# A smaller first wave and a reordered start in a two-layer feed-forward and convolution kernel with 4-bit weights

## The chip, the cores and the metric

The kernel runs on one core of a Trainium2 chip. The metric is the device time of one execution in microseconds (us); several executions of one kernel agree to within a fraction of a per cent. The core has five engines that run side by side, each with its own queue of instructions that it works through in order: TensorE (PE in the profile; its weight loads are PEld), VectorE (DVE), ScalarE (ACT), GpSimd (POOL) and SyncE (SP). SP, ACT and POOL also issue DMA transfers, and such an issue stands in the engine's queue like any instruction: if it waits, what is behind it waits too.

## The reference

The input is 2048 rows of 1024 numbers. Three residual steps follow each other: half a gated feed-forward layer, a long convolution along each row (an S4 kernel made from small tables), and the same feed-forward layer once more. Each normalises its rows first. The weights of the feed-forward layer are 4-bit numbers, eight to a word, with a zero point and a scale for each group of 128 input rows.

```python
def _layernorm(x, axis=-1, eps=1e-05):
    m = jnp.mean(x, axis=axis, keepdims=True)
    v = jnp.var(x, axis=axis, keepdims=True)
    return (x - m) / jnp.sqrt(v + eps)

# in _dequant: 4-bit weights, W[k,n] = scales[g,n] * (w4[k,n] - (z4[g,n]+1))
w = (qw[:, None, :] >> shifts[None, :, None] & MAXQ).reshape(-1, qweight.shape[1])
z = ((qz[:, :, None] >> shifts[None, None, :] & MAXQ) + 1).reshape(qzeros.shape[0], -1)
return (w.astype(scales.dtype) - z[g_idx].astype(scales.dtype)) * s

# in _L0_ffn_ref: 1024 -> 2752 (gate and up) -> 1024 (down)
h = jax.nn.silu(xf @ Wg) * (xf @ Wu)
out = h @ Wd

# the whole
x = x + 0.5 * ffn(_layernorm(x))
x = x + s4_convolution(_layernorm(x))
x = x + 0.5 * ffn(_layernorm(x))
```

## The kernel before

The 2048 rows are four blocks of 512, and the two feed-forward layers make eight jobs of one block and one layer (`JOBS`, L1260). A job has two stages, `gate_up` and `down`. In `gate_up` the 2752 columns of gate and up are taken in pairs of 128 columns (one of gate, one of up): 21 pairs and a half one. Pairs are grouped in waves (`WAVES`, L37): five waves of three pairs and three of two, the last with the half pair. A wave holds one PSUM bank of 128x512 for each of its six (or four) units and goes through the eight groups of 128 input rows; wave and group are a step (`STEPS`), 64 in all. In a step every unit gets two products, the high part of the rows (`xTh`) and the low part (`xTl`), and then its bank is multiplied in place by the ratio of two groups' scales (`scaled`, L596). ScalarE does the gate units, VectorE the up units; in job 0 ScalarE takes one up unit too in every fourth step. I call that an eviction. At the wave's end come silu, the product of gate and up, and the split of the result in two parts (`gated`, L653).

Weights are unpacked once, in job 0. For a wave `fetch` loads the packed words (tile `raw`), `fetch_zeros` reads zero points spread over rows from a DRAM table (`z`), `split` makes two tiles of bytes (`even` and `raw`, L453 and L454), `take_zeros` adds the zero points (L461 and L462), and `dequantize` (L474) casts one of eight interleaved rows at a time to a tile `q` and stores it to the DRAM tensor `wq` of the wave. From there each step's weights come back as bytes (`load_bytes`, L550, four steps ahead) and are cast to 32 bits (`make_weights`, L567, three steps ahead) into `w_up`. The very first step's bytes are put together directly in the tile `first_tile`, by eight small DMAs on POOL's queue. `zero_words` (L263) and `zero_points` (L277) load the packed zero points (`zq`), unpack them (`zi`), and store the table (`ztab` to `z_dram` or `zd_dram`).

Before job 0 stands `start` (L1379): it loads the first four row tiles `x_0` to `x_3`, finds mean and variance (`moments`, `deviations`), unpacks wave 0, normalises the first half of the columns (`less_mean` and `by_deviation` on ScalarE, `turn` with transposes on TensorE, `xTh` on ScalarE, `xTl` on VectorE, L242), and makes the scales of the first three pairs (`scales`, L316). `in_order_of_writing` (L140) holds the instructions of ACT, VectorE and SP in the order in which `start` has them. The other work is placed by a scheduler when the kernel is built, which can move instructions on an engine past each other.

Side work hangs on steps: the dictionaries `up` and `dn` name what is written out at the start of which step. In job 0 the second half of the rows (`second_half`) hangs on steps 0 to 3, the scales of pairs 3 to 8 on step 2, and the unpacking of wave w on the steps from 8w-12 on. In the jobs that follow a first layer (jobs 1, 2, 5 and 6) the block before gets its last additions at steps 0 to 3 (`back`, L709), its moments and deviations at steps 4 and 5, and its convolution from step 8 (in job 1 from step 38). In jobs 3 and 4 the next block's moments and deviations hang on steps 44 and 45.

Pools matter in one place: `qpool` has four buffers, and a tile `q` is free again only when both of its DMAs have landed.

Of the kernel before, what the change touches and what calls it, by code (L numbers as in the profile page):

```python
# [36 lines left out]
WAVES = [list(range(3 * w, 3 * w + 3)) for w in range(5)] + [[15, 16], [17, 18], [19, 20]]  # L37
# [17 lines left out]
def macaron_s4_kernel(  # L55
# [207 lines left out]
    def zero_words(which):  # L263

        if which:
            n = HID // 8 // SEGD
            z = t2("zq_1").bitcast(I32)[: GD * SEGD, :n]
            nc.sync.dma_start(z, down_qz.rearrange("g (s n) -> (g s) n", s=SEGD))
            return z
        n = INTER // 8 // SEG  # L270
        z = t2("zq_0").bitcast(I32)[:, :n]
        for i, src in enumerate((gate_qz, up_qz)):
            own = slice(GK * SEG * i, GK * SEG * (i + 1))
            nc.scalar.dma_start(z[own], src.rearrange("g (s n) -> (g s) n", s=SEG))
        return z
# [198 lines left out]
    def dequantize(w, j):  # L474

        q = qpool.tile([P, width_of(w)], I8, tag="q", name=f"q_{w}_{j}")
        engine = nc.vector if w == 0 and j % 3 < 2 else nc.gpsimd
        engine.tensor_copy(q, packed[w][j % 2][:, j // 2, :])
        dst = w_q[w].rearrange("(r j) n -> j r n", j=8)[j]
        if w == 0:  # L480
            nc.gpsimd.dma_start(first_tile[j:P:8], q[: P // 8])
        nc.sync.dma_start(dst, q)
        if j == 7:
            packed.pop(w)

# [81 lines left out]
    def make_weights(i):  # L567
# [5 lines left out]
        elif j == 0 and stage == "up" and s % GK in (1, 2, 5):  # L573
            nc.scalar.copy(t, b)
        else:
            nc.gpsimd.tensor_copy(t, b)  # L576
# [3 lines left out]
    def next_weights():  # L580
        i = at_use[0]
        at_use[0] += 1
        for k in range(LOAD) if i == 0 else ():
            load_bytes(k)
        for k in range(MAKE) if i == 0 else ():
# [676 lines left out]
    def fast():  # L1262
        for j, (b, k) in enumerate(JOBS):
# [50 lines left out]
            if j == 0:  # L1314
# [6 lines left out]
                at(up, 40, scales_down)  # L1321
                for t in range(NT):
# [56 lines left out]
    def start():  # L1379
        zeros = zero_words(0)  # L1380
        x[0] = [t4(f"x_0_{t}") for t in range(NT)]
        for t, src in enumerate(rows_of(u, 0)):
            (nc.sync, nc.scalar)[t // 2].dma_start(x[0][t], src)
        fetch(0)
# [4 lines left out]
        zero_points(0, zeros)  # L1389
        fetch_zeros(0)  # L1390
        fetch_zeros(1)

        def then(t, m):
            means[t] = m
            less_mean(t, 0)
            if t == 2:
                split(0)
# [4 lines left out]
        for i in range(8):  # L1402
            dequantize(0, i)
        for t in range(NT + 1):
            if t < NT:
                by_deviation(t, 0)
            if t:
                turn(0, t - 1, first[t - 1, 0], 0)
        for t in range(NT):
            less_mean(t, 1)  # L1410
        scales(0, 3, srow)
        zero_points(1, zeros_down)
        return rows_next

    srow_next = in_order_of_writing(start, *STARTING)
# [88 lines left out]
```

## Time and profile before

| | |
|---|---|
| median of 3 executions | 2164.68 us (2164.53 to 2165.5) |
| the profiled execution, own time | 2165.84 us |
| its span in the profile | 2164.1 us |
| mean granted TensorE clock | 0.993 |
| PE busy | 2097.0 us, 97% of the span |
| DVE busy | 1723.0 us, 80% |
| ACT busy | 1422.9 us, 66% |
| POOL busy | 1038.7 us, 48% |

The span is the time from the first to the last recorded instruction; the execution's own time has a little around it. A share of busy time is an average over stages with different limits, so the text below reads single stretches: a window of the timeline, or the waits of one engine. In a timeline line the first number is the start in us from the span's start, the second how long the group took, then come engine, source line, operation, what is written from what is read, the shape, and in brackets the idle time before it with what ended it. L numbers are lines of the kernel before.

Where TensorE waits for nothing it takes 0.22 to 0.23 us for each product of 128x128 by 128x512.

### The profile page before, as it was taken

The page shows a single profiled execution, that of the slowest core. Times are in us where ns is not written, and L with a number is a line of the kernel's source. Part 1 is how long each engine was busy: PE and PEld are TensorE (multiplying, and loading weights), DVE is VectorE, ACT ScalarE, POOL GpSimd, SP SyncE. Part 2 cuts the span into 40 slices and gives each one's busy share as a digit, 9 for nine tenths or more (in the row PEclk, how much of TensorE's full clock was granted, in tenths as well). Part 3 has the DMA queues.
Part 4 walks back from the last instruction along what each step waited for, and adds up shares of the span by engine and source line. Part 5 has one row for each costly group of instructions (what it writes and reads, how often), then busy time and mean ns, then how long its engine had stood idle before and what let it go on. Part 6 is the DMA issues. An engine that isn't in the chain of part 4 may idle for free.

```text
span 2164.1 us, 30241 instructions
## 1 busy us (share of the span) xinstructions
PE 2097.0 (97%) x9748; PEld 1429.4 (66%) x9748; DVE 1723.0 (80%) x2831; ACT 1422.9 (66%) x2233; POOL 1038.7 (48%) x1366
## 2 busy tenths in 40 slices
PE   5999899899999999999999999999999999999998
PEld 3555676476867568665776558676686766866576
DVE  7889787778887877778777787878778787777776
ACT  5887677546754677676667767646776467767765
POOL 3868835444345453455335553445534455345642
PEclk9999999999999999999999999999999999999999
DMA  4433321112111311211321121112111121121111
GB/s 141 122 95 116 113 65 42 43 46 80 37 39 51 97 45 46 80 34 33 111 76 42 31 72 35 41 52 74 37 34 40 54 93 44 47 81 36 33 35 57
DMA packets 163543, 132.48 MB, mean 61 GB/s; under 512 B 22252, under 2 KB 151029, under 8 KB 163376
## 3 DMA queue, kind: packets, MB, share of 16 engines
q1 hardware_dynamic: 162528, 129.12, 19.7%
q8 instruction: 79, 1.29, 0.3%
q10 hardware_dynamic: 592, 1.25, 0.2%
q14 instruction: 88, 0.72, 0.1%
q0 software_dynamic: 256, 0.10, 0.0%
HBM read 104.79 MB, written 25.50 MB: 60 GB/s over the span
## 4 chain that ended last, share of the span: by engine, by line
PE 86%; DVE 8%; DMA 2%; POOL 2%; issue 1%; ACT 0%; SPq 0%; DVEq 0%; POOLq 0%; ACTq 0%
PE pg L628 52%; PE po L691 27%; PE pc L993 3%; DVE pg L600 2%; PE pb L713 1%; PE pb L993 1%; DVE po L600 1%; PE pt L219 1%; PE st L219 1%; DVE hf L658 1%; POOL qd L510 1%; DMA raw<-in_L_ffn_up_qweight_dram 0%; PE s_k L915 0%; ACT g L655 0%; DVE hb L674 0%
## 5 line engine op out<-in xcount | busy, mean ns | idle before, releaser
L598 ACT ACTIVATE pg<-pg,rat 128x512 f32<-128x512 f32 x1240 | 786.5, 660 | 435.7 <-PE pg L628 435.0
L600 DVE TENSOR_TENSOR pg<-pg,rat 128x512 f32<-128x512 f32 x1168 | 776.2, 693 | 168.3 <-PE pg L628 163.5
L628 PE MATMUL pg<-xTh,w_up 128*128 128x512 f32 x2752 | 855.1, 438 | 8.3 <-DVE pg L600 6.0
L628 PE MATMUL pg<-xTl,w_up 128*128 128x512 f16 x2752 | 722.8, 383 | 12.4 <-DVE w_up L572 6.6
L576 POOL CAST w_up<-b 128x768 fp32r<-128x768 int8 (+2 forms) x487 | 375.2, 775 | 566.6 <-PE pg L628 454.9
L628 PEld LDWEIGHTS pg<-xTh,w_up 128*128 128x128 f32 x2752 | 519.7, 189 | 185.1 <-DVE pg L600 23.3
L691 PE MATMUL po<-hl,w_down 128*128 128x512 f32 x1344 | 542.7, 406 | 15.5 <-DVE po L600 11.4
L598 ACT ACTIVATE po<-po,ratd 128x512 f32<-128x512 f32 x660 | 431.9, 662 | 167.7 <-PE po L691 167.3
L691 PE MATMUL po<-hh,w_down 128*128 128x512 f32 x1344 | 525.9, 393 | 0.0
L600 DVE TENSOR_TENSOR po<-po,ratd 128x512 f32<-128x512 f32 x620 | 427.1, 697 | 94.1 <-PE po L691 89.9
L628 PEld LDWEIGHTS <-w_up 128*128 128x128 bf16 x2752 | 228.6, 99 | 336.5 <-issue 152.5
L576 POOL CAST w_down<-bd 128x512 fp32r<-128x512 int8 x352 | 222.6, 634 | 417.8 <-PE po L691 357.8
L691 PEld LDWEIGHTS po<-hl,w_down 128*128 128x128 f32 x1344 | 253.9, 189 | 91.9 <-DVE po L600 24.3
L691 PEld LDWEIGHTS po<-hh,w_down 128*128 128x128 f32 x1344 | 254.7, 190 | 45.8
L662 POOL TENSOR_TENSOR hl<-hf,hh 128x512 fp32r<-128x512 f32 x168 | 217.4, 1294 | 8.4
L658 DVE SCALAR_TENSOR_TENSOR hf<-pg,rat,g 128x512 f32<-128x512 f32 x168 | 123.2, 748 | 45.0 <-ACT g L655 39.9
L655 ACT ACTIVATE g<-pg,rat 128x512 f32<-128x512 f32 x168 | 110.8, 687 | 51.2 <-PE pg L628 41.1
L660 POOL CAST hh<-hf 128x512 fp32r<-128x512 f32 x168 | 106.2, 632 | 63.3 <-PE pg L628 37.1
L182 DVE BATCH_NORM_STATS2 stats<-x 128x6 f32<-128x512 f32 x96 | 63.3, 675 | 0.4
L1023 DVE TENSOR_TENSOR x<-x,pc 128x512 f32<-128x512 f32 x32 | 22.0, 686 | 36.4 <-PE pc L993 36.4
L219 PE MATMUL pt<-ident,xn 128*128 128x128 f32 x256 | 43.8, 288 | 7.3 <-ACT xn L1371 7.3
L242 DVE TENSOR_TENSOR xTl<-pt,xTh 128x512 f16<-128x512 f32 x56 | 38.3, 688 | 13.7 <-ACT xTh L241 12.9
(177 smaller groups left out, 1047.8 us busy)
## 6 DMA issues: line engine op xcount, KB each, us to landing
b<-wq SPq DMA_DIRECT2D x319, 96.0 KB
bd<-wdq SPq DMA_DIRECT2D x336, 64.0 KB
x<-in_L_attn_u_dram SPq DMA_DIRECT2D x30, 512.0 KB
b<-wq SPq DMA_DIRECT2D x128, 64.0 KB
xs<-x SPq DMA_DIRECT2D x16, 512.0 KB
x<-xs SPq DMA_DIRECT2D x16, 512.0 KB
out_dram<-x SPq DMA_DIRECT2D x16, 512.0 KB
b<-wq SPq DMA_DIRECT2D x64, 80.0 KB
```

Source lines behind the costliest of these rows:

```text
L182: nc.vector.bn_stats(stats[:, t, i, :], x[b][t][:, bass.ts(i, 512)])
L219: nc.tensor.transpose(ps[:, bass.ts(k, P)], n[:, bass.ts(k, P)], ident)
L576: nc.gpsimd.tensor_copy(t, b)
L598: nc.scalar.activation(dst, src, AF.Copy, scale=sc)
L600: nc.vector.tensor_tensor(dst, src, sc.to_broadcast([P, TB]), ALU.mult)
L628: nc.tensor.matmul(p, weights, (lo, hi)[k][:, g, :], start=(g == 0 and not done), stop=(g == GK - 1 and done), skip_group_check=True,)
L655: nc.scalar.activation(g, pg, AF.Silu, scale=rat[:, 2 * f, GK - 1 :])
L658: nc.vector.scalar_tensor_tensor(hf, pu, last, g, ALU.mult, ALU.mult)
L660: nc.gpsimd.tensor_copy(hi, hf)
L662: nc.gpsimd.tensor_tensor(lo, hf, hi.bitcast(F32), ALU.subtract)
L691: nc.tensor.matmul(ps[c], w[:, bass.ts(c, P)], part, start=(f == 0 and k == 0), stop=(f == NF - 1), skip_group_check=True,)
L993: nc.tensor.matmul(dst, lhsT, rhs, start=start, stop=stop, skip_group_check=True)
```

## The change

The waves are regrouped: the first one now has two pairs, five have three, and the last two have two. Before, the first five had three and the last three had two. Their number stays eight.

In `start` the packed zero points are loaded first, one half on SP's queue and one on ACT's; then the words of wave 0; then the rows, three tiles on SP's queue and one on ACT's (before, two on each, ahead of the words). The zero points of wave 0 are unpacked and its words split before the moments, not around them. A one-element silu right behind the first DMA issues makes ScalarE load its function table there.

Wave 0 is cast by a function of its own, `dequantize_first`: two rows of eight on GpSimd and six on VectorE, as before, but in another order, in pairs that share a tile of the h pool instead of `qpool`; both the small DMAs to `first_tile` and the stores to `wq` go by SP, the latter four instead of eight. The first step's bytes and weights are written at the end of `start`, ahead of the scales; of the next steps' casts, step 1's goes to GpSimd instead of ScalarE. The zero points for down are unpacked at step 12 of job 0 instead of in `start`.

```diff
-WAVES = [list(range(3 * w, 3 * w + 3)) for w in range(5)] + [[15, 16], [17, 18], [19, 20]]
+WAVES = [[0, 1]] + [list(range(3 * w - 1, 3 * w + 2)) for w in range(1, 6)] + [[17, 18], [19, 20]]
...
-        for i, src in enumerate((gate_qz, up_qz)):
+        for i, (src, queue) in enumerate(((gate_qz, nc.sync), (up_qz, nc.scalar))):
             own = slice(GK * SEG * i, GK * SEG * (i + 1))
-            nc.scalar.dma_start(z[own], src.rearrange("g (s n) -> (g s) n", s=SEG))
+            queue.dma_start(z[own], src.rearrange("g (s n) -> (g s) n", s=SEG))
...
-        engine = nc.vector if w == 0 and j % 3 < 2 else nc.gpsimd
-        engine.tensor_copy(q, packed[w][j % 2][:, j // 2, :])
-        dst = w_q[w].rearrange("(r j) n -> j r n", j=8)[j]
-        if w == 0:
-            nc.gpsimd.dma_start(first_tile[j:P:8], q[: P // 8])
-        nc.sync.dma_start(dst, q)
+        nc.gpsimd.tensor_copy(q, packed[w][j % 2][:, j // 2, :])
+        nc.sync.dma_start(w_q[w].rearrange("(r j) n -> j r n", j=8)[j], q)
         if j == 7:
             packed.pop(w)
+
+    def dequantize_first():
+
+        n = width_of(0)
+        dst = w_q[0].rearrange("(r j) n -> r j n", j=8)
+        parts = packed.pop(0)
+        for j in (0, 1, 5, 4):
+            q = t2(f"q_0_{j}").bitcast(I8)[:, : 2 * n].rearrange("p (i n) -> p i n", i=2)
+            for i in range(2):
+                row = j + 2 * i
+                engine = nc.vector if j else nc.gpsimd
+                engine.tensor_copy(q[:, i], parts[j % 2][:, row // 2, :])
+                nc.sync.dma_start(first_tile[row:P:8], q[: P // 8, i])
+            nc.sync.dma_start(dst[:, j : j + 3 : 2], q)
...
-        elif j == 0 and stage == "up" and s % GK in (1, 2, 5):
+        elif j == 0 and stage == "up" and s > 1 and s % GK in (1, 2, 5):
...
-        for k in range(LOAD) if i == 0 else ():
+        for k in range(1, LOAD) if i == 0 else ():
             load_bytes(k)
-        for k in range(MAKE) if i == 0 else ():
+        for k in range(1, MAKE) if i == 0 else ():
             make_weights(k)
...
+                zeros = lambda: zero_points(1, zeros_down)
+                at(up, 12, lambda: in_order_of_writing(zeros, ET.DVE, ET.SP))
...
     def start():
         zeros = zero_words(0)
+        fetch(0)
         x[0] = [t4(f"x_0_{t}") for t in range(NT)]
         for t, src in enumerate(rows_of(u, 0)):
-            (nc.sync, nc.scalar)[t // 2].dma_start(x[0][t], src)
-        fetch(0)
+            (nc.sync, nc.scalar)[t // 3].dma_start(x[0][t], src)
+        warm = small.tile([P, 1], F32, tag="warm", name="warm")
+        nc.gpsimd.memset(warm, 0.0)
+        nc.scalar.activation(warm, warm, AF.Silu)
+        zero_points(0, zeros)
+        split(0)
+        fetch_zeros(0)
         srow = scale_rows(0, 3)
         zeros_down = zero_words(1)
         fetch(1)
         rows_next = scale_rows(3, 9)
-        zero_points(0, zeros)
-        fetch_zeros(0)
         fetch_zeros(1)
 
         def then(t, m):
             means[t] = m
             less_mean(t, 0)
-            if t == 2:
-                split(0)
 
         moments(0, 1, then)
         deviations(0, 1, -LIFT)
         take_zeros(0)
-        for i in range(8):
-            dequantize(0, i)
+        dequantize_first()
         for t in range(NT + 1):
             if t < NT:
                 by_deviation(t, 0)
             if t:
                 turn(0, t - 1, first[t - 1, 0], 0)
+        load_bytes(0)
+        make_weights(0)
         for t in range(NT):
             less_mean(t, 1)
         scales(0, 3, srow)
-        zero_points(1, zeros_down)
-        return rows_next
+        return rows_next, zeros_down
```

More of the change, by code (lines that the diff above doesn't have):

```diff
@@ L1411, in start @@
         scales(0, 3, srow)
[L1412 to L1415 removed]
+        return rows_next, zeros_down
+    srow_next, zeros_down = in_order_of_writing(start, *STARTING)
     x.pop(0)
```

## The prediction

> **What bounds the kernel now.** I read the page's shares first, then the chain of waits, then the two ends of the change: the first 60 us, and the first wave of a later job.
>
> ```profile
> PE 86%; DVE 8%; DMA 2%; POOL 2%; issue 1%; ACT 0%; SPq 0%; DVEq 0%; POOLq 0%; ACTq 0%
> ```
>
> That is the chain that ended last: TensorE carries 86% of the span and VectorE 8%. Outside the start TensorE is the bound, so a change of the start is worth what it lets TensorE begin and keep its pace earlier. The waits of TensorE, then of VectorE, in the first 62 us (total, times, longest):
>
> ```profile
> PE pg L628 <- DVE w_up L572: 6.6, 1, 6.6
> PE pg L628 <- POOL w_up L576: 0.8, 1, 0.8
> ```
> ```profile
> DVE zi L282 <- DMA zq<-in_L_ffn_up_qzeros_dram: 6.4, 1, 6.4
> DVE q L478 <- DMA b<-q: 2.1, 2, 1.6
> ```
>
> The first product waits for its weights, which VectorE casts. VectorE's own timeline (start, duration) says why they are late:
>
> ```profile
> 6.40 0.84 DVE L282 TENSOR_SCALAR zi<-zq 128x43 int32<-128x43 int32 x8 [6.40 <-DMA zq<-in_L_ffn_up_qzeros_dram]
> ...
> 7.71 1.28 DVE L182 BATCH_NORM_STATS2 stats<-x 128x6 f32<-128x512 f32 x2
> ...
> 16.89 0.17 DVE L205 TENSOR_SCALAR r<-r 128x4 f32<-128x4 f32 x1
> 17.07 0.96 DVE L461 TENSOR_TENSOR even<-even,z 128x1536 uint16<-128x1536 uint16 x1
> ...
> 23.62 0.56 DVE L478 COPY q<-even 128x768 int8<-128x768 int8 x1 [1.64 <-DMA b<-q]
> ...
> 25.69 2.47 DVE L242 TENSOR_TENSOR xTl<-pt,xTh 128x512 f16<-128x512 f32 x4
> ...
> 28.51 0.56 DVE L572 CAST w_up<-b 128x768 fp32r<-128x768 int8 x1
> ```
>
> VectorE sits idle until 6.40, waiting for 22 KB of packed zero points, and from there works without a gap but for the 2.1 us at 23-25. After the first product it is still VectorE that sets the pace. Windows over TensorE's products of L628 (length, busy and number), one window for each of the first three waves of 96 products:
>
> ```profile
> 29.10:59.90 30.80, 27.22 (x96) 0.94 0.41 120
> 59.90:83.00 23.10, 22.54 (x97) 1.00 0.42 124
> 83.00:104.70 21.70, 21.70 (x97) 1.00 0.36 103
> ```
>
> The third wave runs at 21.7/96 = 0.226 us a product, TensorE's own pace; the first needs 30.8. The second thing to see is a later job's first wave, in windows over all engines (length; PE, PEld, DVE, ACT, POOL busy):
>
> ```profile
> 1376.00:1392.00 16.00, 16.00 (x75) 9.87 (x72) 15.75 (x38) 10.52 (x18) 4.78 (x6) 1.00 0.12 32
> ```
>
> VectorE is 15.75 of 16 us busy there, beside a TensorE that is never idle: no room is left.
>
> [...] here the last store of `wq` is issued at 25.80 and the load that needs it at 27.82, 2.02 later. [...] the zero points, issued at 0.75 and 1.33 on ACT's queue, come only at 6.40 with a megabyte of rows on SP's queue beside them. [...] the trace has 1.28 us at 10.82 and at 56.34. [...] the cast q<-even took 1.49 us at 18.68 beside VectorE and 0.83 at 24.06.
>
> **The change part by part.**
>
> *Loads.* The two zero-point loads are now first on SP and ACT, then the words (2 x 128 KB instead of 2 x 192), then x_0 to x_2 on SP and x_3 on ACT. With nothing ahead, the zero points cost about the 2 us: at 2.9 instead of 6.4 (estimate). The DMA moved 322 and 353 GB/s in its busiest slices; 2.1 MB of x and 0.26 MB of words at 0.35 MB/us after a start at 1.5 give x_2 at about 8.4, words at 4.3, x_0 at 5.6. VectorE: zero points 1.4 (0.84+0.52) to 4.3, split of 512 columns 0.75 to 5.1, then moments of 1.34 each as rows come: x_2 done at 9.8, x_3 at 11.1, against 14.5. Bounds: 10 if rows come sooner[...]. The 2.55 us of deviations follow: 13.7 against 17.07. z is stored right after 4.3 and read by about 10, so it is not late.
>
> *Casts of the first wave.* take_zeros on 512 columns costs two thirds of 3.5 us, 2.3: to 16.0. Six casts on VectorE stay six, each 0.37 instead of 0.55: 18.3. The 2.1 us of waits for a buffer of `q` go, as four tiles of the h pool hold the results. Then the four xTl, 2.4: 20.7; ScalarE's last xTh lay 6.2 after r, so 19.9, and doesn't hold them. Late next is SP: the 12 stores (8 to `first_tile`, formerly on POOL's queue, and 4 to `wq`) at 0.45 to 0.5 each, the first after POOL's cast at about 15.9, put the last `first_tile` store at 20.6 and the last `wq` store at 21.2. Landing takes 1.7 to 2: 22.4. The cast of the first weights, 0.4, ends at 22.9 (bounds 21.5 and 24.2), against 29.07: 6.2 us earlier. `b` of step 1 is read after the last `wq`, 23.2, lands at 25, and POOL casts it by 25.5; step 0 is 8 products, 1.8 us, and the first eviction waits for the scales anyway, so this costs about nothing.
>
> *First wave.* It shrinks to 64 products, 14.5 us of TensorE. VectorE's work from the first weights to the wave's last eviction, in pitches from the first 60 us: scales 3.4 (both sets now stand ahead of the first eviction), 12 evictions at 0.6, four xTl 2.4, splits and zeros of waves 1 and 2 at 4.4 each, less a last step of 0.6: about 20. Before, the same list had 19 evictions and the zero points of down. So 22.9+20 = 42.9, and about 2.5 more because wave 2's z, issued behind four `wq` stores at about 37, lands near 41.7 with two evictions queued behind that wait (in the trace such a z, issued at 45.33, ended a wait at 49.76). POOL's cast of step 8's weights stands behind the first cast of wave 2, so wave 1 begins near 46.2. Add 32 products at wave 1's 0.24: 96 products done at 53.9 instead of 59.9. **Start: -6.0** (bounds -3.5 and -8.5).
>
> *Zero points of down* move to step 12: 1.2 us of VectorE in wave 1, in pieces of 0.1. VectorE had 20.3 busy of 23 us there, so most is covered: +0.4 (0 to 1.2).
>
> *ACT table.* The load at 10.82 ended before the rows' means were all there, and the one at 56.34 fell where TensorE did not wait: 0. One load for all is enough, since one stands in the built program.
>
> *Order of waves, all 8 jobs.* Products stay 688 a job. The pair wave leaves place 5 and comes to place 0, so hooks by step number meet other steps. In jobs 2, 5 and 6 the moments and deviations of the block before (step 4 on) now lie in steps of 1.8 us. The built program puts three statistics of 0.6 and two aggregates between two evictions there, 2.0 us, where a two-pair step allows about 1.1: +1 each, less the shorter knot at the wave's end (bounds -0.5, +2): +3. Job 1 has the same runs of VectorE work between evictions as before: 0 (bounds -2, +2). The other way round, jobs 3 and 4 hold the next block's moments at step 44, formerly in pair waves:
>
> ```profile
> 1233.20:1265.20 32.00, 30.87 (x129) 1.00 0.13 36
> 1507.90:1537.20 29.30, 29.30 (x130) 1.00 0.15 39
> ```
>
> The first is job 4's two pair waves with moments, the second job 5's without: 2.7 us lost. In a three-pair wave part of that is covered: -0.8 each, -1.6. Job 0's pair wave in place 5 took 15.7 us for 64 products (a window from 148.6), 1.2 over pace; with 21.6 us to hide the same splits: -1. Sum of the order: +0.4.
>
> Sum: -6.0+0.4+0.4 = **-5.2 us**. Against the profiled execution's own 2165.84 (span 2164.1) that is 2160.6; that execution lay 1.16 over the median of 2164.68, so on the median **2159.5**.
>
> **Rivals.**
> (A) As summed: 2159.5, own range 2156 to 2163. Chance 0.55.
> (B) The first product comes early, but a new wait takes half: SP's 12 stores, z of wave 2, or POOL's order in front of step 8. For it: VectorE's evictions already stand behind a wait for z once (0.3 us). Against: six microseconds of VectorE work are really gone or moved. Gain 2 to 3: 2162. Chance 0.17.
> (C) Slower: the two-pair wave at each job's head. VectorE was full there with 2.7 us steps; with 1.8 us steps the four additions, the moments and the transposes stall TensorE. Without the +3 for it the sum is -8.2, so it cancels the change at 1.2 us for each of 7 jobs and makes it slower by 0.2% from 1.8; at 2.0 us each it is -8.2+14.0, 2170.5. Against: evictions per product are the same and the transposes, 0.44 us a step, give slack. Chance 0.17.
> (D) The start gains more, as rows and casts come without contention, and the tail of job 0 loses a knot: -9, 2155.7. Chance 0.11.
>
> **How the numbers follow.** The measurement can tell about 0.2%, 4.3 us: faster means below 2160.35, slower above 2169.0. A lies two thirds on the faster side, D wholly; B and the rest of A are within; C is mostly beyond. Faster 0.50, same 0.34, slower 0.16. Range 2154.5 to 2167: A, B, D and the lower part of C.
>
> **What would show it.** Right: zi starts near 3, r ends near 14, the first cast w_up near 22.5, no wait q<-b, 64 products by about 46. Wrong: a first cast after 24.5; a first wave over 25 us; job 5's first 64 products above 17.5 us (14.5 and 1.8 of transposes are 16.3), or job 3's above 16.5.

## The result, and the profile after

The changed kernel takes 2180.77 us (median of 4 executions, 2177.65 to 2183.03), the kernel before 2164.98 in the same runs. The ratio is 1.0072 with an interval of 1.0054 to 1.0089: slower, by about 16 us. The prediction, 2159.5 with a range up to 2167, was wrong in sign. The profiled execution took 2180.45 us, its span is 2178.2, 14.1 longer than the span before. One of the four executions of one kernel below (waves alone) took 4270.38 us and is left out of its median.

The chain of waits hardly changed, so it can't tell where the time went:

```profile
PE 86%; DVE 9%; DMA 2%; POOL 1%; issue 1%; ACT 1%; SPq 1%; DVEq 0%; POOLq 0%; ACTq 0%
```

Waits of the changed kernel in the first 62 us (engine, what waited, for whom: total, times, longest), first TensorE's, then VectorE's:

```profile
...
PE pg L638 <- DVE pg L610: 3.6, 3, 2.0
PE pg L638 <- DVE w_up L582: 2.7, 1, 2.7
...
PE pg L638 <- POOL w_up L586: 1.1, 1, 1.1
```
```profile
...
DVE zi L282 <- DMA zq<-in_L_ffn_up_qzeros_dram: 3.3, 1, 3.3
DVE w_up L582 <- DMA b<-q: 1.7, 1, 1.7
...
DVE even L461 <- DMA z<-z_dram: 1.4, 1, 1.4
```

The wait for the first weights fell from 6.6 to 2.7 us, and the wait `q<-b` is gone, as intended. But TensorE now waits 3.6 us for evictions, and VectorE for zero points. VectorE's timeline shows how late the first weights still are:

```profile
3.33 0.84 DVE L282 TENSOR_SCALAR zi<-zq 128x43 int32<-128x43 int32 x8 [3.33 <-DMA zq<-in_L_ffn_up_qzeros_dram]
...
8.14 1.29 DVE L182 BATCH_NORM_STATS2 stats<-x 128x6 f32<-128x512 f32 x2 [1.39 <-DMA x<-in_L_attn_u_dram]
...
16.35 0.17 DVE L205 TENSOR_SCALAR r<-r 128x4 f32<-128x4 f32 x1
...
26.87 0.43 DVE L582 CAST w_up<-b 128x512 fp32r<-128x512 int8 x1 [1.74 <-DMA b<-q]
```

The zero points come 3.1 us earlier than before, the variances (`r`) only 0.5, the first weights 1.6. The first three waves, in windows over TensorE's products (length, busy and number, weight loads, granted clock, DMA share, GB/s), begin at 27.4, 53.9 and 81.4:

```profile
27.40:53.90 26.50, 19.54 (x64) 8.97 (x65) 0.98 0.33 96
53.90:81.40 27.50, 24.13 (x97) 12.94 (x97) 0.96 0.41 118
81.40:103.30 21.90, 21.90 (x97) 12.65 (x96) 1.00 0.46 135
```

So 160 products are done at 81.4. The kernel before had 96 at 59.9 and 192 at 83.0, which at its 0.241 us a product is 160 at 75.3. It began 1.7 us later and was 6.1 ahead there.

I found the rest by noting when each job's first product starts:

| | before | changed | difference |
|---|---|---|---|
| job 0 | 29.1 | 27.4 | -1.7 |
| job 1 | 304.1 | 307.8 | +3.7 |
| job 2 | 605.4 | 611.4 | +6.0 |
| job 3 | 878.7 | 888.3 | +9.6 |
| job 4 | 1123.2 | 1133.0 | +9.8 |
| job 5 | 1368.9 | 1377.9 | +9.0 |
| job 6 | 1640.6 | 1651.7 | +11.1 |
| job 7 | 1912.4 | 1927.2 | +14.8 |
| end of span | 2164.1 | 2178.2 | +14.1 |

Jobs 0 and 1 lose 6.0 us together. Of the later ones, which lose 8.1 together, jobs 2, 5 and 6 lose 3.6, 2.1 and 3.7, the others nothing. In windows over all engines (PE, PEld, DVE, ACT, POOL busy, granted clock), job 6's first two waves before, and the same of jobs 6 and 5 after:

```profile
1640.60:1664.60 24.00, 24.00 (x114) 14.96 (x114) 22.68 (x50) 15.50 (x26) 6.89 (x9) 1.00 0.14 38
1664.60:1696.20 31.60, 31.60 (x175) 22.99 (x174) 25.39 (x41) 17.05 (x27) 18.98 (x23) 1.00 0.14 43
```
```profile
1651.70:1668.40 16.70, 16.70 (x81) 9.96 (x81) 15.59 (x33) 10.83 (x17) 5.59 (x9) 1.00 0.17 46
1668.40:1703.90 35.50, 33.52 (x175) 23.83 (x174) 28.63 (x49) 17.20 (x27) 17.43 (x22) 0.95 0.13 41
...
1394.60:1428.50 33.90, 31.94 (x176) 22.94 (x175) 28.29 (x49) 17.12 (x27) 17.34 (x22) 1.00 0.14 43
```

TensorE is idle 1.98 and 1.96 us in these second waves after (35.5 less 33.52; 33.9 less 31.94) and never before. The first waves, where I had put the cost, run full.

### The profile page after: what moved, and what is told of

Same layout as the page of the kernel before. It is cut to its first block, busy times and chain, and to the rows that moved or that the text cites. A ratio compares the mean times of both kernels' runs of the same rounds, so it can differ in the third digit from the quotient of the medians.

```text
span 2178.2 us, 30204 instructions
## 1 busy us (share of the span) xinstructions
PE 2100.1 (96%) x9748; PEld 1426.4 (65%) x9748; DVE 1724.0 (79%) x2831; ACT 1421.9 (65%) x2232; POOL 1034.9 (48%) x1360
## 4 chain that ended last, share of the span: by engine, by line
PE 86%; DVE 9%; DMA 2%; POOL 1%; issue 1%; ACT 1%; SPq 1%; DVEq 0%; POOLq 0%; ACTq 0%
PE pg L638 52%; PE po L701 26%; PE pc L1003 3%; DVE pg L610 2%; PE pb L723 1%; PE pb L1003 1%; DVE po L610 1%; PE pt L219 1%; PE st L219 1%; DVE hf L668 1%; DVE rawd L461 0%; DMA z<-z_dram 0%; ACT g L665 0%; POOL hl L672 0%; DVE xn L212 0%
## 5 line engine op out<-in xcount | busy, mean ns | idle before, releaser
L701 PE MATMUL po<-hl,w_down 128*128 128x512 f32 x1344 | 541.2, 405 | 15.2 <-DVE po L610 10.8
L672 POOL TENSOR_TENSOR hl<-hf,hh 128x512 fp32r<-128x512 f32 x168 | 217.8, 1296 | 8.6
L242 DVE TENSOR_TENSOR xTl<-pt,xTh 128x512 f16<-128x512 f32 x56 | 38.3, 688 | 13.7 <-ACT xTh L241 12.9
L1003 PEld LDWEIGHTS pc<-near,st 128*128 128x128 f32 x256 | 43.6, 190 | 7.9
```

Of the source, the lines that this page charges most:

```text
L672: nc.gpsimd.tensor_tensor(lo, hf, hi.bitcast(F32), ALU.subtract)
L701: nc.tensor.matmul(ps[c], w[:, bass.ts(c, P)], part, start=(f == 0 and k == 0), stop=(f == NF - 1), skip_group_check=True,)
L1003: nc.tensor.matmul(dst, lhsT, rhs, start=start, stop=stop, skip_group_check=True)
```

## The experiments

For each kernel: when the first product, job 1 and job 2 start and the span ends in its profiled execution, the difference of the last two, and the median of all its executions. The kernel before had 2164.54 to 2165.48 in these runs.

| kernel | first product | job 1 | job 2 | end | jobs 2 to 7 | median |
|---|---|---|---|---|---|---|
| before | 29.1 | 304.1 | 605.4 | 2164.1 | 1558.7 | |
| changed | 27.4 | 307.8 | 611.4 | 2178.2 | 1566.8 | 2180.77 |
| waves alone | 27.4 | 309.1 | 611.3 | 2175.3 | 1564.0 | 2178.21 |
| start alone | 29.0 | 303.2 | 607.0 | 2165.6 | 1558.6 | 2167.37 |
| pair wave late | 27.3 | 310.9 | 615.1 | 2174.2 | 1559.1 | 2176.69 |
| small stores on POOL | 25.1 | 313.5 | 615.5 | 2179.6 | 1564.1 | 2184.25 |
| loads for wave 2 first | 26.9 | 307.4 | 609.6 | 2175.7 | 1566.1 | 2179.22 |
| convolution later | 27.4 | 313.6 | 615.6 | 2181.6 | 1566.0 | 2181.75 |
| moments later too | 27.2 | 312.4 | 614.4 | 2186.3 | 1571.9 | 2189.29 |
| down's splits as written | 26.9 | 308.2 | 608.9 | 2172.9 | 1564.0 | 2178.27 |
| the same, pair wave late | 26.9 | 310.0 | 609.6 | 2169.3 | 1559.7 | 2169.85 |
| down's splits in a row, pair wave late | 27.0 | 304.4 | 608.5 | 2167.2 | 1558.7 | 2169.81 |
| results split off GpSimd | 27.0 | 307.9 | 610.8 | 2169.4 | 1558.6 | 2171.63 |
| changed, all mended | 27.0 | 303.2 | 606.7 | 2166.3 | 1559.6 | 2168.99 |
| old waves, stores on POOL | 26.7 | 301.4 | 605.2 | 2164.1 | 1558.9 | 2165.41 |
| the same, job 1's moments later | 27.4 | 307.6 | 605.3 | 2164.2 | 1558.9 | 2166.03 |
| the same, job 1's results off GpSimd | 27.4 | 302.1 | 604.3 | 2164.1 | 1559.8 | 2165.59 |

The column "job 1" needs care. In most kernels four products of job 1 are placed among the last of job 0, whose own last product starts 6.4 us after job 1's first. In three kernels fewer are: the two with down's splits as written, and the one with job 1's moments later. TensorE at the end of job 0 in the kernel before, and in the last of these three:

```profile
304.06 0.39 PE L628 MATMUL pg<-xTl,w_up 128*128 128x512 f16 x1
...
310.49 0.39 PE L691 MATMUL po<-hb,w_down 128*128 128x512 f32 x1
```
```profile
307.56 0.39 PE L638 MATMUL pg<-xTl,w_up 128*128 128x512 f16 x1
...
308.25 0.39 PE L701 MATMUL po<-hb,w_down 128*128 128x512 f32 x1
```

By job 0's last product, which starts at 310.5 before and 314.3 in the changed kernel, the three (311.3, 313.0 and 308.2) lie 0.8 and 2.5 us behind the kernel before and 2.3 ahead of it.

**Waves or start.** The first kernel is the one before with the new `WAVES` alone, the second the changed one with the old line:

```diff
-WAVES = [[0, 1]] + [list(range(3 * w - 1, 3 * w + 2)) for w in range(1, 6)] + [[17, 18], [19, 20]]
+WAVES = [list(range(3 * w, 3 * w + 3)) for w in range(5)] + [[15, 16], [17, 18], [19, 20]]
```

> The kernel before with the new list of waves and nothing else of the change. Theory P (the pair wave at the head is what costs: some 11 us in jobs 1, 2, 5 and 6, and in job 0 it is too short to hide the unpacking of waves 1 and 2): about 2178 (2174 to 2181). Theory S (the reordered start costs, with 12 stores in a row on SP and late zero points; the order of waves costs little): 2163 to 2168.

> The changed kernel with the old list of waves, so all of the change but the regrouping. Theory P: about 2165 (2163 to 2168), jobs 1 to 7 as long as before. Theory S: 2174 to 2179, first product later than 29.1 us.

The waves alone cost 0.62% (0.42 to 0.82%), the new start alone 0.10% (0.03 to 0.17%). Both totals lie in theory P's ranges and outside S's, so the loss belongs to the regrouped waves. And the start, which I had counted at -6 us together with the shorter wave, gains nothing: with waves of three pairs its first product comes at 29.0, as before. Even the 1.7 us of the changed kernel come from the smaller wave, as the waves alone show (27.4).

**The pair wave in sixth place from job 1 on.** Job 0 stays as changed.

```diff
+LATER = [(w, g) for w in (1, 2, 3, 4, 5, 0, 6, 7) for g in range(GK)]
...
-            w, g = STEPS[s]
+            w, g = (LATER if j else STEPS)[s]
...
-        for s, (wi, g) in enumerate(STEPS):
+        for s, (wi, g) in enumerate(LATER if j else STEPS):
```

> The changed kernel; jobs 1 to 7 visit the pair wave 0 in sixth place, job 0 is as in the changed kernel. Theory P: the jobs' share of the loss, 11 us, goes: about 2170 (2168 to 2172), and job 0 stays about 5 us behind. Theory S, or a loss from the regrouping that has nothing to do with the place of the wave in a job: 2179 to 2182.

Jobs 2 to 7 are back at 1559.1 us. The median fell by only 4.1, and 2176.69 lies outside both ranges: in the profiled execution job 0 took 3.1 us longer than in the changed kernel. Job 0 spreads that much by itself: the changed kernel and three kernels below (convolution later, moments later too, results split off GpSimd) have the same instructions up to job 2's first wave, and their job 1 started at 307.8, 313.6, 312.4 and 307.9. So I read the late share from the column of jobs 2 to 7, and job 1's start with caution.

**The first weights earlier.** The eight small stores to `first_tile` go by POOL's queue again.

```diff
-                nc.sync.dma_start(first_tile[row:P:8], q[: P // 8, i])
+                nc.gpsimd.dma_start(first_tile[row:P:8], q[: P // 8, i])
```

> The changed kernel with the eight stores to first_tile back on POOL's queue; SP keeps four to wq. Both theories: the first weights come earlier than 26.9 us if SP's row of 12 issues of 0.62 us holds them; about 25. Theory S: the total falls by as much or more, to 2176 to 2179. Theory P: what follows in job 0 waits for the unpacking of waves 1 and 2 and takes most of it back: 2179 to 2181.

The first product came 2.3 us earlier, and job 1 5.7 later than in the changed kernel; the median, 2184.25, is above what both theories expected. The first wave took 30.0 us (25.1 to 55.1) instead of 26.5, with a wait of TensorE at its end whose like takes 1.1 us at most in the changed kernel:

```profile
PE pg L638 <- POOL w_up L586: 5.8, 1, 5.8
```

It is for the second wave's first weights, which GpSimd casts behind its first cast of wave 2. So an earlier first product is worth nothing by itself here; the next paragraphs follow what the second wave waits for.

**What slows job 0's second wave.** In the changed kernel SP's own timeline has the loads for wave 2, from 42.98 us on, behind wave 1's first four stores (39.41 to 42.93), which wait for GpSimd's casts:

```profile
27.66 3.55 SPq L568 DMA_DIRECT2D b<-wq  x7
39.41 3.52 SPq L478 DMA_DIRECT2D wq<-q  x4
42.98 0.42 SPq L440 DMA_DIRECT2D raw<-_L_ffn_gate_qweight_dram  x1
43.45 0.43 SPq L440 DMA_DIRECT2D raw<-in_L_ffn_up_qweight_dram  x1
43.92 1.28 SPq L447 DMA_DIRECT2D z<-z_dram  x2
```

VectorE needs the zero points at 47.7 and gets them at 49.17; TensorE, and GpSimd's cast that stands ahead of the next weights, wait behind it (timelines of VectorE and TensorE):

```profile
49.17 0.96 DVE L461 TENSOR_TENSOR even<-even,z 128x1536 uint16<-128x1536 uint16 x1 [1.43 <-DMA z<-z_dram]
50.05 0.69 DVE L610 TENSOR_TENSOR pg<-pg,rat 128x512 f32<-128x512 f32 x1
```
```profile
50.79 0.38 PE L638 MATMUL pg<-xTl,w_up 128*128 128x512 f16 x1 [2.02 <-DVE pg L610]
52.73 0.72 PE L638 MATMUL pg<-xTh,w_up 128*128 128x512 f32 x1 [1.32 <-DVE pg L610]
```

The kernel before has the same order (its `z` is issued at 44.68), but its first wave lasts until 59.9, so the same chain meets the middle of a wave. The experiment loads wave 2 at step 0 and the later waves three steps earlier:

```diff
-                at(up, s0 - 3, lambda both=both: in_order_of_writing(both, ET.SP))
+                if w > 2:
+                    at(up, s0 - 6, lambda both=both: in_order_of_writing(both, ET.SP))
...
+                both = lambda: (fetch(2), fetch_zeros(2))
+                at(up, 0, lambda both=both: in_order_of_writing(both, ET.SP))
                 both = lambda: (split(1), take_zeros(1))
```

> The changed kernel, with the words and zero points of wave 2 loaded at step 0, ahead of wave 1's eight stores on SP's queue, and those of waves 3 to 7 three steps earlier. Theory K (in job 0 the unpacking of the next waves is a chain that runs through SP: VectorE's bytes of wave 1, POOL's casts, SP's stores of wave 1, and only behind them the loads for wave 2, on which VectorE waits with evictions queued behind it): VectorE's waits for z and raw between 27 and 84 us (4.7 us together in the changed kernel) go to under 1, the first 160 products end near 77 us instead of 81.4, job 1 starts near 304 instead of 307.8, total 2175 to 2178. Theory V (VectorE's and GpSimd's amount of unpacking work sets the pace of the first waves): the waits move elsewhere, 160 products end at 80 to 82, total 2179 to 2183.

VectorE's waits for `z` and `raw` between 27 and 84 us, 4.7 us in the changed kernel, are gone; one wait is left, for TensorE:

```profile
DVE pg L613 <- PE pg L641: 6.9, 10, 1.7
```

160 products were done at 78.0 instead of 81.4, so theory K holds for the first two waves. But job 1 started at 307.4, and the median of 2179.22 lies in V's range. Of the 3.4 us gained, the seventh wave (steps 48 to 55) gave back 1.8 (20.4 us instead of 18.6), the sixth wave and the second stage the rest.

**The seventh wave.** In the kernel with the convolution later (below), whose job 0 is that of the changed kernel, VectorE's and TensorE's timelines show why that wave is long:

```profile
186.27 0.42 DVE L453 TENSOR_SCALAR rawd<-rawd 88x512 int32<-88x512 int32 x1 [4.47 <-DMA rawd<-_L_ffn_down_qweight_dram]
```
```profile
187.35 0.79 PE L638 MATMUL pg<-xTh,w_up 128*128 128x512 f32 x1 [4.89 <-DVE pg L610]
```

The first operation on the third tile of down's words was placed ahead of most of the second tile's and of evictions, and its load is late. In the changed kernel's own profile the same wait is 2.03 us. Two edits move that operation back, both on top of the earlier loads. One holds the splits in the order of writing against everything on VectorE; it ran with the changed order of waves and with the pair wave late. The other holds them only one behind the other; it ran with the pair wave late (`in_a_row` is a helper of that kernel: the first instruction on VectorE of each split waits for the last one of the split before):

```diff
-                at(*when(max(0, n - 1)), lambda a=a, rt=rt: split_down(a, rt))
+                halves = lambda a=a, rt=rt: split_down(a, rt)
+                at(*when(max(0, n - 1)), lambda halves=halves: in_order_of_writing(halves, ET.DVE))
```
```diff
-                at(*when(max(0, n - 1)), lambda a=a, rt=rt: split_down(a, rt))
+                at(*when(max(0, n - 1)), lambda a=a, rt=rt: in_a_row(lambda: split_down(a, rt)))
```

> The changed kernel with the earlier loads of wave 2 onwards (as in the run with the words of wave 2 first), and besides the splits of down's words held on VectorE in the order in which they are written, so that the first operation on the third tile no longer stands ahead of the second tile's and of several evictions. Theory K2 (job 0's seventh wave, steps 48 to 55, is long because VectorE stands at that operation until its words land, 2.0 us in the changed kernel and 4.5 in another run of the same instructions, with evictions behind it): the wave's 64 products take at most 17.5 us (18.6 in the changed kernel, 20.4 with the earlier loads alone, up to 23.6 elsewhere), no wait of VectorE for rawd there, job 1 starts at 303.5 to 305.5, total 2173 to 2177. Rival G (GpSimd: with a three-pair wave in sixth place six instead of four operations that split h stand ahead of the casts of w_up): the wave stays at 19 us or more, total 2177 to 2181.

> The same, and from job 1 on the pair wave in sixth place (job 0 keeps the changed order). It is the closing sum: if three things make up the loss (SP's order in front of wave 2, the splits of down, and the pair wave at the head of jobs 1 to 7), job 1 starts at 303.5 to 305.5, jobs 2 to 7 have the stages of the kernel before, job 1 about 2 us more (it had 2.2 to 2.9 more in every kernel with the new start), and the total is 2164 to 2168, no difference from the kernel before or at most 0.15% over it. If something unnamed is left, it stays at 2170 or more. A gain over the kernel before isn't expected by any theory: the first product is 2 us earlier, and job 1 takes 2 us more.

> The earlier loads of wave 2 onwards, the pair wave in sixth place from job 1 on, and the splits of down's words chained one tile after another on VectorE, but free against everything else. Holding them in the order of writing had put the third tile's split at 218 instead of 199 us, its stores came late (GpSimd's casts ready at 225 instead of 208), and TensorE waited in job 0's second stage (106 us instead of 99). Theory K3 (job 0's loss is VectorE's waits for late loads with evictions behind, and the second stage was hurt only by that late third tile): the seventh wave's 64 products take at most 17.5 us, the second stage 98 to 101 us again, job 1 starts at 302.5 to 305.5, total 2164 to 2167.5. Theory U (the unpacking of down, not TensorE, ends job 0, and with the new first wave it is done later): the wave is short, but the second stage takes it back, job 1 starts at 307 or later, total 2168 to 2172.

Held in the order of writing, the wave took 14.9 us and VectorE no longer waited for `rawd` there: K2 holds for the wave, G falls. But the third tile was then split only by 218.6 us instead of 199.0, and job 0's second stage was longer, 109.4 us from its first product to its last instead of 105.4, with a wait of TensorE that isn't in the changed kernel's list from 189 to 308 us (here 190 to 308):

```profile
PE po L705 <- POOL w_down L590: 5.2, 4, 1.9
```

The totals that the expectations put at 2173 to 2177 and at 2164 to 2168 were missed, with 2178.27 (in G's range, though not by G's wave) and 2169.85. Chained in a row, the wave took 16.9 us, the second stage up to job 1's first product 98.6, and job 1 started at 304.4, within 0.3 of the kernel before: K3 in all its profiled numbers, though the median of 2169.81 lies 2.3 above what K3 expected, in U's range. Job 1 itself took 304.1 us against 301.3. These are single profiled executions; the medians agree that job 0 was mended, as the pair wave late alone had 2176.69.

**Jobs 2, 5 and 6.** I first took the transposes' deadline for the cause, then the short steps:

```diff
-                    late = 30 if j == 1 else 0
+                    late = 30 if j == 1 else 3
```
```diff
-                    at(up, 4, lambda: moments(pb, 2))
-                    at(up, 5, lambda: deviations(pb, 2))
+                    at(up, 4 if j == 1 else 9, lambda: moments(pb, 2))
+                    at(up, 5 if j == 1 else 10, lambda: deviations(pb, 2))
```

The second kernel also has the convolution six steps later.

> The changed kernel, with the convolution hooks of jobs 2, 5 and 6 three steps later (normalise from step 11, transposes from 13, and so on); moments and deviations stay at steps 4 and 5. Theory D (deadline: TensorE's transposes at step 10 come before VectorE has the normalised rows, since step 10 is now 5 us nearer to step 4): the up stages of jobs 2, 5 and 6 fall from 191.6, 190.4 and 190.1 us to about 188, total 2171 to 2174. Theory C (crowding: the deviations' chain of tiny operations sits between evictions of 1.8 us steps and delays them, wherever the transposes stand): at most 1 us back in each, total 2178 to 2182.

> The changed kernel, with moments and deviations of jobs 2, 5 and 6 at steps 9 and 10 (in the first wave of three pairs) instead of 4 and 5, and the convolution six steps later. Theory C (crowding in the short steps of the pair wave): the up stages of jobs 2, 5 and 6 come back to 187 to 188 us, total 2170 to 2173, at least as good as with the convolution alone moved. Theory D (deadline): the same 2171 to 2174, so this kernel tells C from D only beside the one with the convolution alone moved. A third case, that the last additions of the block before (steps 0 to 3) are what stalls the pair wave: both kernels stay within 2 us of the changed one.

(The changed kernel's stages are 191.6, 188.3 and 190.0; the 190.4 for job 5 in the first of these is off.) With the convolution later the stages are 192.1, 188.1 and 188.2, and TensorE is still idle 1.65 us in job 5's second wave: D falls. With the moments in a three-pair wave they are 192.3, 191.0 and 191.0, and TensorE is idle twice: C falls too, and the third case, as the median is 8.5 us over the changed kernel's. Windows of that kernel over job 5's second and fifth wave:

```profile
1399.20:1424.60 25.40, 23.49 (x105) 13.80 (x105) 21.87 (x40) 16.08 (x26) 11.73 (x14) 1.00 0.13 36
1495.20:1519.30 24.10, 22.26 (x98) 12.99 (x97) 23.05 (x44) 15.23 (x25) 12.15 (x15) 1.00 0.26 82
```

In these places the deviations (of the second norm, and in the fifth wave of the third) run on past the end of a wave, and TensorE is idle 1.65 to 1.98 us. What is there at a wave's end is GpSimd, which splits `h` and casts weights without a pause. Set beside each other, VectorE's deviations in job 6 of the changed kernel and GpSimd's timeline:

```profile
1671.56 0.62 DVE L204 SCALAR_TENSOR_TENSOR r<-e,r 128x4 f32<-128x4 f32 x1
...
1672.70 0.80 DVE L202 TENSOR_TENSOR e<-r 128x4 f32<-128x4 f32 x1
1673.53 1.20 DVE L203 TENSOR_TENSOR e<-e,ve 128x4 f32<-128x4 f32 x1
```
```profile
1670.89 1.27 POOL L672 TENSOR_TENSOR hl<-hf,hh 128x512 fp32r<-128x512 f32 x1
...
1672.65 0.83 POOL L586 CAST w_up<-b 128x768 fp32r<-128x768 int8 x1
1673.44 1.26 POOL L672 TENSOR_TENSOR hl<-hf,hh 128x512 fp32r<-128x512 f32 x1
```

Start plus duration: VectorE's three end at 1672.18, 1673.50 and 1674.73, GpSimd's at 1672.16, 1673.48 and 1674.70. Operations of four numbers a row, which take 0.16 us in `start`, stand here until GpSimd's operation is over, and evictions and TensorE stand behind them: that is theory H of the next experiment. What makes them wait no trace shows. The evictions keep their 0.68 to 0.70 us beside GpSimd. In the kernel before single casts of GpSimd hold the deviations up too (in job 6 one takes 0.73 us and ends at 1660.11, the cast at 1660.10), but they are over at 1663.78, before the splits begin at 1665.63, and TensorE doesn't wait. The experiment takes GpSimd away at that place and gives VectorE more to do:

```diff
+        if j in (2, 5, 6) and f < 2:
+            nc.scalar.copy(hi, hf)
+            nc.vector.tensor_tensor(lo, hf, hi.bitcast(F32), ALU.subtract)
+        else:
             nc.gpsimd.tensor_copy(hi, hf)
             nc.gpsimd.tensor_tensor(lo, hf, hi.bitcast(F32), ALU.subtract)
```

> The changed kernel; in jobs 2, 5 and 6 the two results of the first wave are split on ScalarE (high part) and VectorE (low part) instead of GpSimd. Theory H ([...] in job 6 of the changed kernel the operations of the deviations that took 0.62, 0.80 and 1.20 us end at 1672.18, 1673.50 and 1674.73, and GpSimd's operations at 1672.16, 1673.48 and 1674.70): with GpSimd nearly free at the wave's end these operations fall to 0.15 to 0.3 us (one or two may still meet a cast of w_up), TensorE's idle in the second wave of job 5 falls from 1.98 to under 1 us, the jobs 2 to 7 take 1558 to 1562 us together instead of 1566.8, total 2172 to 2177. Theory Q (the operations only queue behind evictions, the amount of VectorE work decides): VectorE has 1.4 us more to do there, the idle stays at 2 us or grows, jobs 2 to 7 take 1567 or more, total 2179 to 2185.

```profile
1667.13 0.15 DVE L202 TENSOR_TENSOR e<-r 128x4 f32<-128x4 f32 x1
...
1667.80 0.14 DVE L203 TENSOR_TENSOR e<-e,ve 128x4 f32<-128x4 f32 x1
...
1668.47 0.15 DVE L204 SCALAR_TENSOR_TENSOR r<-e,r 128x4 f32<-128x4 f32 x1
```

The operations take 0.15 us, TensorE's idle in that wave is 0.41 in job 6 as in job 5, and VectorE, which now does more, is busy 27.35 us in job 5's second wave instead of 28.29. Jobs 2 to 7 take 1558.6 us, as in the kernel before, and the median is 9.1 lower than the changed kernel's, a little more than H expected. Theory H holds and Q, which had the opposite sign, falls.

**The sum, and versions with the old waves.** All mended, with the new order of waves in every job:

> The changed kernel with its order of waves in all jobs, the earlier loads of wave 2 onwards, the splits of down's words chained on VectorE, and the first wave's results split off GpSimd in jobs 1, 2, 5 and 6. If the three causes named are the whole loss and theory H holds: job 1 starts at 302.5 to 305.5, jobs 2 to 7 take 1558 to 1562, total 2164 to 2170. With theory Q 2175 or more.

2168.99 us, 0.22% (0.12 to 0.32%) over the kernel before: 11.8 of some 16 us are found, and all three figures lie in the expected ranges. Three more kernels have the old waves, the new start, the small stores on POOL's queue, and scale rows and words of wave 1 loaded ahead of SP's wait. The second also moves job 1's moments, the third splits job 1's first results off GpSimd with the edit above for `j == 1 and f < 3`:

```diff
-        fetch_zeros(0)
         srow = scale_rows(0, 3)
+        fetch(1)
+        fetch_zeros(0)
         zeros_down = zero_words(1)
-        fetch(1)
```
```diff
-                    at(up, 4, lambda: moments(pb, 2))
-                    at(up, 5, lambda: deviations(pb, 2))
+                    at(up, 17 if j == 1 else 4, lambda: moments(pb, 2))
+                    at(up, 18 if j == 1 else 5, lambda: deviations(pb, 2))
```

> The changed kernel's start with the waves of the kernel before, the eight small stores to first_tile on POOL's queue again, and the loads of the scale rows and of wave 1's words ahead of SP's wait for the zero point table. Theory K/P (a reordered start can gain, once SP's row of twelve stores is broken up, as the wave behind it is long enough for the unpacking): first product at 26 to 27 us (29.0 with the twelve stores on SP), job 1 starts 1 to 3 us earlier than 303.2, total 2162 to 2165.5, at or slightly under the kernel before. Theory V (VectorE's work up to the end of job 0 sets it): the first product comes early, the first wave is longer by as much, total 2165 to 2168.

> The old waves with the new start and the small stores on POOL's queue (2165.41), and job 1's moments and deviations hung on steps 17 and 18 (third wave) instead of 4 and 5. That kernel had job 1 start 2.7 us earlier than the kernel before (301.4 against 304.1) and lost 2.5 in job 1 (217.8 against 215.3), where VectorE's tiny operations of the deviations fall between a reciprocal and the evictions at the end of the first wave (TensorE waits 1.28 us). If that knot is the cause, job 1's first stage comes to 214 to 216 and the total to 2161 to 2163.5, faster than the kernel before by 0.05 to 0.15%. If the third wave has no room either, job 1 stays at 217 to 219 and the total at 2164.5 to 2167.

> The old waves with the new start and the small stores on POOL's queue (2165.41), and in job 1 the three results of the first wave split on ScalarE and VectorE. There the last operation of the deviations took 1.14 us, to 335.60, beside a GpSimd operation to 335.57, and TensorE waited 1.28 us behind it. Theory H: that wait goes, job 1 takes 1 to 2 us less than 303.8, job 2 starts at 603 to 604.5, total 2162.5 to 2164.5, under the kernel before by at most 0.1%. Theory Q: job 2 starts at 605 or later, 2165 or more.

Their ratios are 1.0002 (0.9993 to 1.0010), 1.0005 (0.9997 to 1.0013) and 1.0002 (0.9994 to 1.0011). The first median lies in the ranges of both theories; the other two are above what the causes under test would have given. The first product comes 1.7 to 2.4 us earlier than before, and job 0's last product starts 2.0 to 2.6 us earlier (307.9, 308.2 and 308.5 against 310.5; the 307.6 in the table is the mark that moved). But job 2 starts at 604.3 to 605.3, against 605.4: most of what job 0 gains, job 1 gives back. In the first of the three job 1's first stage takes 217.8 us instead of 215.3, with TensorE idle 10.3 us instead of 9.2 and busy 207.5 instead of 206.1. Why, wasn't tried. Theory H's gain in job 1 is there in the profile (302.2 us instead of 303.8) but not in the median. No version beats the kernel before.

## Why the prediction was wrong, point by point

Two terms of the sum failed. "Start: -6.0" reckoned with one wait of 2.5 us behind the first weights, where a chain of loads and stores runs through SP's queue: 96 products were done at 62.2 us instead of 53.9 (59.9 before), and job 0 ended 3.7 us late. "Order of waves: +0.4" priced the moments and deviations at the head of a job by durations of operations that nothing disturbs, +1 us in each of three jobs: jobs 2 to 7 lost 8.1. The other 2.3 us lie in job 1, and their cause stays open.

*Bound and direction.* That TensorE ends the chain and VectorE sets the pace of the start was right. The step from there, that earlier weights are time gained, failed, as the small stores on POOL's queue show.

*Loads.* Zero points at 2.9: measured 3.33. The rows failed: x_0 was put at 5.6, and the first statistics waited for it until 8.14. In the trace the packets of x_0 to x_2 move from 4.9 to 10.6 on SP's queue, behind the words, and x_0 is through at 7.7. x_3, alone on ACT's queue, is through at 5.1, but the statistics take x_0 first. From there the durations were right (5.8 us to the last aggregate, 2.5 for the deviations), so `r` came at 16.5 instead of 13.7. "z is stored right after 4.3 and read by about 10, so it is not late" held for VectorE, but not for SP: the store was issued at 4.75, and SP's next instruction, the read of z, came at 11.17, 6.4 us later, where it had been 2.0 before (10.39 to 12.35).

*Casts of the first wave.* The wait for a buffer of `q` went, as said. SP's row of stores was mis-sized: 0.45 to 0.5 us each was taken, they came every 0.63 (18.68 to 25.56 for eleven steps). With 2.8 us from the rows, 2.1 from the stores, and 0.4 less for the landing, the first cast ended at 27.3 instead of 22.9. Two marks for "wrong" were passed: a first cast after 24.5, and a first wave over 25 us.

*First wave.* 23.3 us from first weights to its end were predicted, 26.5 measured. The wait for wave 2's z was seen, at 2.5 us, but not that it is one of a chain: the next wave ran at 0.287 us a product instead of 0.24. So "Start: -6.0" became +2.3 at 96 products (62.2 against 59.9) and +6.1 at 160. At the end of the first stage it was +6.5 (208.9 against 202.4), and the second stage, 98.9 us up to job 1's first product instead of 101.7, left 3.7. The seventh wave cost 0.9 in this execution (18.6 us against 17.7) and up to 6 in others. With the loads of wave 2 and the splits of down's words mended, job 1 started at 304.4.

*Zero points of down, ACT table.* +0.4 can't be told apart in the second wave. The table is loaded once, in 1.28 us at 2.25, and cost nothing, as ScalarE's first work on the rows came at 9.70.

*Order of waves.* Jobs 3 and 4 were to gain 0.8 each: measured +0.2 and -0.8. Jobs 2, 5 and 6 were to lose 1 each, measured 3.6, 2.1 and 3.7. The place, the deviations of the block before, was right; the mark set for it, 17.5 us for job 5's first wave, wasn't reached (16.7), as the loss came in the second wave. The price failed because I counted durations of operations that run undisturbed: 0.15 us each, where beside GpSimd some took 0.62 to 1.20, left TensorE idle for 2.0 us, and in jobs 2 and 6 some 3.4 us at half the granted clock followed (last section). Job 0's "-1" for its pair wave in the old sixth place failed too: the three-pair wave there took 22.9 us, still 1.2 over the wave before it.

*Rivals.* B named the right places in job 0 (SP's twelve stores, wave 2's `z`), but as half of a gain, where they made a loss. C, the slower one, was the right side: +14.1 in the span. It kept a gain of 8.2 from the rest of the change, so it stopped at 2170.5, and its mechanism was near but not right. It charged the four additions and each of seven jobs; the runs charge only the deviations, only where they meet GpSimd at a wave's end, in three jobs.

*What stays open.* About 4 us of the median with all mended. The profiled execution shows 2.2 of them: job 1 loses 2.2 (303.5 us against 301.3) and jobs 2 to 7 lose 0.9, while job 1 starts 0.9 earlier. What orders the work of job 1 between these kernels wasn't settled, nor why job 0's seventh wave spreads from 18.3 to 23.7 us between executions of the same instructions.

## What to carry to other kernels

Before pricing an earlier start, list what must be ready for the second and third piece of work and through which queue it comes (here SP's, where the loads for wave 2 stood behind stores until 42.98 us); a shorter first piece shortens the cover of all of it. Where tiny dependent VectorE operations are placed, look at what GpSimd does at that moment, not at how full VectorE is: here operations of 0.15 us took up to 1.20. End times that coincide to 0.03 us gave this wait away, and it isn't in the list of waits. Compare the start of each job or stage first; it showed within one table that half of this loss lay far from the lines that were argued about. And see that the mark means the same in each kernel: a few products moved by the scheduler shifted it here by more than 5 us.

## What the runs showed of the hardware

In two of three jobs TensorE's idle cost more than its own time. Job 6 lost 1.6 us more than job 5 in the same wave (35.5 against 33.9) with about the same idle time (1.98 and 1.96 us). Windows over TensorE behind that idle, in the changed kernel (length, busy and number, granted clock):

```profile
1672.00:1676.00 4.00, 2.62 (x11) 1.00 0.09 25
1676.00:1680.00 4.00, 3.40 (x14) 0.70 0.09 25
1680.00:1684.00 4.00, 4.00 (x17) 0.88 0.09 25
1684.00:1688.00 4.00, 4.00 (x25) 1.00 0.11 30
```

The granted clock fell to 0.70 and 0.88 for 8 us, which is 4.00 x 0.30 + 4.00 x 0.12 = 1.7 us; in job 5 it stayed at 1.00. In windows of half a microsecond it is 0.50 from 1678.0 to 1680.5, with 0.58 in the one ahead of that and 0.51 in the one behind, which adds up to the same 1.7 us, or about 3.4 us at half the clock. Six products with `xTh` took 3.11 us from 1677.55, and 1.74 from 1681.84. Job 2, with 1.95 us of idle, paid the same (0.50 or 0.51 from 636.5 to 639.5, and 0.58 to 640.0). The three idle times, 5.9 us together, and two such stretches of 1.7 are nearly all of the 9.4 us that jobs 2, 5 and 6 lost. What sets it off wasn't shown: the gaps of TensorE ahead of it were 1.14 and 0.84 us in job 6 and 1.11 and 0.84 in job 2, and in job 5, where the clock stayed at 1.00, they were 1.12 and 0.84.

A small store took three times as long beside a large load of another queue: the store of the zero point table (172 KB, ACT's queue) released its reader 6.4 us after its issue at 4.75, while 1.5 MB of rows moved on SP's queue until 10.6, and 2.0 us after its issue at 10.39 in the kernel before, where the rows were through at 9.6. Its own packets moved from 8.6 to 10.8; before, from 11.2 to 11.8.
